# A VectorE no-op that takes the cross-engine waits of each scan group in a four-layer scan network

## The chip, the cores and the metric

The kernel runs on one core of a Trainium2 chip. A core has a matrix engine (TensorE, PE in the profile), three engines for elementwise work (VectorE = DVE, ScalarE = ACT, GpSimd = POOL) and a queue engine that issues the DMAs (SyncE = SP). [...] The metric is the device time of one execution in microseconds (us), as a median of several.

## What is computed

Four layers on images of 48 x 48 x 192, batch 4, all float32. Layers 0 to 3 are variants of the same thing, a selective scan over a sequence of tokens (layer 0 along 2304 tokens in both directions, layers 1 and 2 in four directions, layer 3 along rows and columns of 48). Cut to what matters here:

```python
delta = softplus(dt @ dtW.T + dtB)         # (L, D)
A = -exp(A_log)                            # (D, N), N = 16 states
def step(h, t):                            # t runs over the L tokens
    d_t, u_t, b_t, c_t = t
    h = exp(d_t[:, None] * A) * h + (d_t * u_t)[:, None] * b_t[None, :]
    return h, sum(h * c_t[None, :], -1)
_, ys = lax.scan(step, h0, (delta, xc, Bm, Cm))
y = ys + xc * D
```

For every channel d and state n there is thus a linear recurrence h = a * h + b over the tokens, with a = exp(delta * A), b = delta * u * B, and then a sum over n of h * C. Projections, short convolutions, norms and gates stand around it.

## The kernel before

**Tiling.** Channels lie on the 128 partitions, in three blocks i = 0, 1, 2. Tokens come in chunks of 384 (`CH`). The 16 states are taken in groups g of four (`NG`), so that one group is a tile of 128 x (4 x 385) or, where the scan starts anew in every row, 128 x (4 x 384). A *job* is one chunk in one direction. In layers 0 and 3 it has 3 x 4 = 12 groups; in layers 1 and 2 (`parts` = 2) two blocks of states share the partitions and a job has 6. Over the kernel there are 3456 groups: 1152 of layer 0, 1152 of layers 1 and 2, 1152 of layer 3.

**One group.** Its steps are methods of `ScanJob`:

- `fetch` (for i = 0 only): a DMA on SP's queue brings B and C of the group, broadcast over the partitions, into a tile `bcb`.
- `decay` (L367): four ScalarE exponentials write the tile `a`, one of three that are used in turn.
- `carry` (L384): in layers 0 to 2 GpSimd copies the state at the end of the chunk before into the first column of `bcb`.
- `enter` (L398), once for each i: ScalarE copies delta * u into the PSUM tile `du`, of which there is one.
- `scan` (L403): VectorE makes the *product* `inputs` = `du` * B (a TENSOR_TENSOR into PSUM) and then the *scan* `h` = scan(`a`, `inputs`) (a TENSOR_TENSOR_SCAN). `inputs` exists once, `h` in three buffers in layer 0 and four elsewhere.
- `weigh` (L421): GpSimd saves the last state (not in layer 3) and multiplies `h` by C in place.
- `reduce` (L435): TensorE sums `h` over the states into `y`, with an identity matrix as weights, four matmuls for a group.

**Order.** `run_jobs` (L737) writes the order out by hand. At step t it records: `scan` of group t, `decay` of group t + 2, `take` of y, `carry` for group t + 1, `weigh` of group t, then pieces of the next job's projections (`stream`) and of a norm (`side`), gates and drives on GpSimd, and `reduce` of group t - 1. `InOrder` (L48) and `in_order` (L95) keep each engine to that order. So GpSimd always has `carry` of group t + 1 just ahead of `weigh` of group t, and TensorE sums a group one step after it was scanned.

**Waits.** Nothing of the waits is written in the kernel: the framework finds for each instruction what it depends on, and leaves out a wait that an earlier instruction of the same engine has made already. [...] In the program as it is built, the stream of VectorE around a typical group of layer 0 reads

```
semaphore instruction   waits DVE (scan before)
TENSOR_TENSOR inputs    waits POOL (carry)
semaphore instruction   waits DVE (this product), PE (readers of the h buffer)
TENSOR_TENSOR_SCAN h    waits ACT (decay)
```

Where POOL and DMA waits are not needed, the product has the DVE wait in its own slot, with no semaphore instruction ahead of it: that is so for 736 of the 3456 products, most of them in layer 3.

Of the kernel before, what the change touches and what calls it, by code (L numbers as in the profile page):

```python
# [13 lines left out]
AF = mybir.ActivationFunctionType  # L14
ALU = mybir.AluOpType
# [11 lines left out]
NG = 4  # L27
# [20 lines left out]
class InOrder:  # L48


    def __init__(self, tc, engine):
        self.tc, self.engine = tc, engine
# [6 lines left out]
class K:  # L59
# [35 lines left out]
    def in_order(self, ins):  # L95
# [9 lines left out]
        self.last_act = ins.ins.name  # L105
        return ins

    def copy(self, out, in_):
        return self.act(out, in_, AF.Copy)

    def mm(self, out, pairs, start=True, stop=True, engine=None):
        n = len(pairs)
        for i, (lhsT, rhs) in enumerate(pairs):
            (engine or self.nc.tensor).matmul(  # L114
                out, lhsT, rhs, start=start and i == 0, stop=stop and i == n - 1
            )

    def mmo(self, out, pairs, start=True, stop=True):

        self.mm(out, pairs, start, stop, self.t)  # L120

    def rsqrt(self, out, in_, eps):

# [99 lines left out]
class ScanPools:  # L223
# [6 lines left out]
    def __init__(self, k, ctx, parts, rows):  # L230
        pool = k.tc.tile_pool
        self.parts, self.rows = parts, rows
        self.wide = 128 // parts
        self.n = N // parts
        self.groups = self.n // NG
        self.W = W = CH if rows else CH + 1
        self.one = ctx.enter_context(pool(name="one", bufs=1))
        self.two = ctx.enter_context(pool(name="two", bufs=2))
        self.bcs = ctx.enter_context(pool(name="bcs", bufs=5 if rows else 4))
        self.hs = ctx.enter_context(pool(name="hs", bufs=4 if rows or parts == 2 else 3))  # L240
        self.y = ctx.enter_context(pool(name="y", bufs=2 if rows else 1, space=PSUM))
        self.ps = ctx.enter_context(pool(name="ps", bufs=2, space=PSUM))
        self.vec = ctx.enter_context(pool(name="vec", bufs=1, space=PSUM))

        inputs = k.tile(self.vec, [128, 1536 if rows else 2048], "inputs")
        self.b = inputs[:, : NG * W].rearrange("p (j l) -> p j l", l=W)
        self.du = k.tile(self.vec, [128, 512], "du")[:, :W]
        self.ones = k.tile(self.one, [128, 1], "ones")
        k.nc.vector.memset(self.ones, 1.0)
        self.decays = [k.tile(self.one, [128, NG, W], f"a{i}") for i in range(3)]  # L250
        self.n_decays = 0
        self.revs = [None] * 3
        self.yts = 3 if rows else 2
        self.rev = None

        self.sum = k.ident
        if parts == 2:
            self.sum = k.tile(self.one, [128, 64], "sum")
            k.nc.vector.tensor_tensor(self.sum, k.ident[:, :64], k.ident[:, 64:], ALU.add)
# [28 lines left out]
class ScanJob:  # L288
# [10 lines left out]
    def __init__(self, k, pools, w, c0, rev, prev):  # L299
        self.k, self.pools, self.w, self.c0, self.rev, self.prev = k, pools, w, c0, rev, prev  # L300
        self.entry, self.tokens = pools.entry(rev)
        self.bcb = {}
        self.y = {}
        self.a = {}
        self.h = {}
        self.du = {}

    def unit(self, slots, rows, pairs, act):

        made = []  # L310

        def pe():
            ps = self.k.tile(self.pools.ps, [128, 512], "ps")[:rows, :CH]
            made.append(ps)
            out, pp = pairs(ps)
            self.k.mmo(out, pp)

        return slots, pe, lambda: act(made[0])
# [36 lines left out]
    def fetch(self, g):  # L355

        k, pools = self.k, self.pools
        wide = pools.wide
        self.bcb[g] = k.tile(pools.bcs, [128, 2, NG, pools.W], "bcb")
        for m in range(pools.parts):  # L360
            at = (m * pools.groups + g) * 2 * NG
            k.nc.sync.dma_start(
                self.bcb[g][m * wide : (m + 1) * wide].rearrange("p s j l -> p (s j l)"),
                self.bc[at : at + 2 * NG, :].rearrange("r l -> (r l)").partition_broadcast(wide),
            )

    def decay(self, i, g, between=None):  # L367

        k, w, pools = self.k, self.w, self.pools
        if i == 0:  # L370
            self.fetch(g)
        a = self.a[i, g] = pools.next_decays(k, self.rev)
        for j in range(NG):
            if j == NG - 1 and between is not None:
                between()
            out, in_ = a[:, j, self.tokens], self.delta[:, i, :]
            if pools.rows:
                lo = 0 if self.rev else 1
                out, in_ = (
                    v.rearrange("p (r l) -> p r l", l=S)[:, :, lo : lo + S - 1] for v in (out, in_)  # L380
                )
            k.act(out, in_, AF.Exp, scale=w.A[:, i, g * NG + j : g * NG + j + 1])

    def carry(self, i, g):  # L384

        if not self.pools.rows and self.prev is not None:
            at = self.entry
            self.k.g.tensor_copy(
                self.bcb[g][:, 0, :, at : at + 1].squeeze(2),
                self.prev.state[:, i, g * NG : (g + 1) * NG],  # L390
            )

    def drive(self, i):

        du = self.du[i] = self.k.tile(self.pools.two, [128, CH], "dus")
        self.k.g.tensor_tensor(du, self.delta[:, i, :], self.xs[:, i, :], ALU.mult)

    def enter(self, i):  # L398

        self.pools.turn(self.k, self.rev)  # L400
        self.k.copy(self.pools.du[:, self.tokens], self.du.pop(i))

    def scan(self, i, g):  # L403

        k, pools = self.k, self.pools
        b, du, W = pools.b, pools.du, pools.W
        k.v.tensor_tensor(
            b, du.unsqueeze(1).to_broadcast([128, NG, W]), self.bcb[g][:, 0, :, :], ALU.mult
        )
        step = -1 if self.rev else 1  # L410
        h = self.h[i, g] = k.tile(pools.hs, [128, NG, W], "h")
        k.v.tensor_tensor_scan(
            h.rearrange("p j l -> p (j l)")[:, ::step],
            self.a.pop((i, g)).rearrange("p j l -> p (j l)")[:, ::step],
            b.rearrange("p j l -> p (j l)")[:, ::step],
            0.0,
            ALU.mult,
            ALU.add,
        )

    def weigh(self, i, g):  # L421

        k, pools = self.k, self.pools
        h = self.h[i, g]
        if not pools.rows:
            if g == 0 and i == 0:
                self.state = k.tile(pools.two, [128, 3, pools.n], "state")
            last = 0 if self.rev else CH
            k.g.tensor_copy(
                self.state[:, i, g * NG : (g + 1) * NG], h[:, :, last : last + 1].squeeze(2)  # L430
            )
        ht = h[:, :, self.tokens]
        k.g.tensor_tensor(ht, ht, self.bcb[g][:, 1, :, self.tokens], ALU.mult)

    def reduce(self, i, g):  # L435

        k, pools = self.k, self.pools
        if g == 0:
            self.y[i] = k.tile(pools.y, [128, 512], "y")[: pools.wide, :CH]
            self.skip(i)  # L440
        h = self.h.pop((i, g))
        for j in range(NG):
            n = g * NG + j
            k.mmo(
                self.y[i],
                [(pools.sum, h[:, j, self.tokens])],
                start=n == 0 and not self.skips,
                stop=n == pools.n - 1,
            )


class DirJob(ScanJob):
# [1382 lines left out]
```

## Time and profile before

| what | value |
|---|---|
| median of 3 runs | 19676.89 us (19675.04 to 19686.36) |
| the profiled execution's own time | 19685.32 us |
| its span, first to last instruction | 19683.5 us |
| granted TensorE clock | 0.942 |
| VectorE busy | 18085.6 us (92%) |
| PE / ACT / POOL busy | 17478.0 (89%) / 12836.3 (65%) / 14746.8 (75%) us |
| HBM traffic | 117 GB/s over the span, queue q1 41.3% of 16 engines |

The first and last groups of the three scan stages start at 36.0 and 6239.1 us (layer 0), 6715.8 and 12941.5 us (layers 1 and 2), 13108.5 and 19221.7 us (layer 3). Between them stand a stage of convolutions and the loading of layer 3, and an MLP comes last.

How to read the profile: a group's line gives line of code, engine, operation, output <- inputs by tile name, shape and number; then busy time, mean ns of one, and after the second bar the idle time of the engine just before those instructions and what ended most of it. As every recorded operation goes through the helper in L56 or L93, tiles tell the groups apart, not lines. A timeline's line gives start, duration, engine, operation, and in brackets the idle time before it, where it is long enough to be named. Semaphore instructions are in the trace, with start and duration, but not in the views.

### The profile page before, as it was taken

How to read it: one execution, taken by the hardware profiler on the slowest of the kernel's cores; microseconds unless marked ns; L12 is line 12 of the kernel's file. 1: busy time of each engine (PE TensorE's matmuls, PEld its weight loads, DVE VectorE, ACT ScalarE, POOL GpSimd, SP SyncE). 2: the span in 40 equal slices, each digit the busy share in tenths (PEclk: the TensorE clock that was granted, in tenths of full speed). 3: DMA queues.
4: the chain of work that ended last, by engine and by line, in shares of the span. 5: the costliest groups of instructions: out<-in, count | busy, mean ns of one | idle time of the engine just before them, and what ended most of it. 6: DMA issues, size and time to landing. Idle time of an engine off the chain costs nothing.

```text
span 19683.5 us, 159587 instructions
## 1 busy us (share of the span) xinstructions
PE 17478.0 (89%) x48240; PEld 8281.7 (42%) x48240; DVE 18085.6 (92%) x7297; ACT 12836.3 (65%) x22582; POOL 14746.8 (75%) x10860
## 2 busy tenths in 40 slices
PE   8999999999998878888888888889999999998989
PEld 4544545444444322233233333334444444444444
DVE  8999999999997699999999999969999999999993
ACT  6766767666665466666666766756666666666663
POOL 7888888878876378888888888857777777777770
PEclk9999999999999989999999999989999999999999
DMA  3333333323323366666666666633222232333221
GB/s 114 115 116 109 118 118 116 116 103 114 115 102 98 95 135 140 148 146 146 146 144 145 138 146 145 138 107 108 105 103 104 105 110 100 110 107 108 104 106 46
DMA packets 500475, 2306.35 MB, mean 117 GB/s; under 512 B 76664, under 2 KB 334304, under 8 KB 347168
## 3 DMA queue, kind: packets, MB, share of 16 engines
q1 hardware_dynamic: 499616, 2296.14, 41.3%
q8 instruction: 387, 6.34, 0.1%
q14 instruction: 472, 3.87, 0.1%
HBM read 2103.60 MB, written 192.32 MB: 117 GB/s over the span
## 4 chain that ended last, share of the span: by engine, by line
DVE 43%; POOL 26%; PE 15%; issue 8%; ACT 5%; DMA 1%; DVEq 1%; POOLq 0%; SPq 0%; ACTq 0%
DVE h L56 28%; POOL h L56 20%; DVE inputs L56 15%; PE y L56 7%; PE ps L56 5%; POOL dus L56 2%; ACT a L93 2%; PE vps L114 2%; POOL state L56 1%; ACT L93 1%; PE mop L114 1%; DMA bcb<-bc 1%; POOL yt L56 1%; PE mps L114 1%; POOL bcb L56 1%
## 5 line engine op out<-in xcount | busy, mean ns | idle before, releaser
L56 POOL TENSOR_TENSOR h<-h,bcb 128x1536 f32<-128x1536 f32 x3456 | 11907.9, 3446 | 1715.9 <-DVE h L56 1440.0
L56 DVE TENSOR_TENSOR_SCAN h<-a,inputs 128x1540 f32<-128x1540 f32 (+1 forms) x3456 | 11609.4, 3359 | 448.2 <-ACT a L93 9.4
L93 ACT ACTIVATE a<-delta,A 128x384 f32<-128x384 f32 (+1 forms) x13824 | 7435.8, 603 | 3166.6 <-DVE h L56 3155.1
L56 PE MATMUL y<-h,ident 128*128 128x384 f32 x18432 | 6776.7, 516 | 509.7 <-POOL h L56 506.3
L56 DVE TENSOR_TENSOR inputs<-du,bcb 128x1540 f32<-128x1540 f32 (+1 forms) x3456 | 6115.4, 1769 | 467.2 <-ACT du L93 88.7
L56 PEld LDWEIGHTS y<-h,ident 128*128 128x128 f32 x18432 | 3620.4, 201 | 3513.4 <-POOL h L56 974.4
L56 PE MATMUL y<-h,sum 128*64 128x384 f32 x9216 | 3652.7, 545 | 595.0 <-POOL h L56 477.7
L56 PEld LDWEIGHTS y<-h,sum 128*64 128x64 f32 x9216 | 1291.4, 150 | 2915.3 <-issue 1756.0
L56 POOL COPY state<-h 128x4 f32<-128x4 f32 x2304 | 431.6, 187 | 2190.7 <-DVE h L56 2144.2
L56 PE MATMUL ps<-xh,diag 128*128 128x384 f32 x4032 | 1419.0, 491 | 185.1 <-ACT xc L93 185.1
L56 PE MATMUL ps<-u,inT 96*128 96x384 f32 x3456 | 1265.6, 497 | 178.8 <-ACT z L93 133.1
L56 PE MATMUL ps<-bcd,dtT 12*128 12x384 f32 (+1 forms) x2304 | 1017.6, 549 | 394.1 <-ACT delta L93 391.2
L56 PEld LDWEIGHTS ps<-xh,diag 128*128 128x128 f32 x4032 | 750.2, 189 | 779.5 <-ACT xc L93 273.2
L93 ACT ACT_TABLE_LOAD x794 | 1018.7, 1283 | 14.6
L90 ACT ACT_TABLE_LOAD x789 | 1012.3, 1283 | 14.7 <-PEq L1825 0.7
L56 PEld LDWEIGHTS ps<-u,inT 96*128 96x128 f32 x3456 | 652.7, 192 | 694.3 <-ACT z L93 211.7
L93 ACT ACTIVATE delta<-ps,vec 128x384 f32<-128x384 f32 x1152 | 631.7, 579 | 298.2 <-PE ps L56 291.2
L56 PE MATMUL ps<-yt,outT 128*96 128x384 f32 x2304 | 789.7, 486 | 0.4 <-POOL yt L56 0.4
L56 PEld LDWEIGHTS ps<-bcd,dtT 12*128 12x128 f32 (+1 forms) x2304 | 383.0, 192 | 965.2 <-ACT delta L93 628.6
L93 ACT ACTIVATE du<-dus 128x384 f32<-128x384 f32 x1152 | 557.9, 484 | 151.3 <-DVE inputs L56 145.8
L56 POOL TENSOR_TENSOR dus<-delta,xc 128x384 f32<-128x384 f32 x576 | 574.7, 998 | 49.8 <-ACT delta L93 49.8
L93 ACT ACTIVATE o<-ps 96x384 f32<-96x384 f32 x288 | 140.3, 487 | 687.8 <-PE ps L56 687.8
(131 smaller groups left out, 9694.4 us busy)
## 6 DMA issues: line engine op xcount, KB each, us to landing
bcb<-bc SPq DMA_DIRECT2D x384, 1540.0 KB
bcb<-bc SPq DMA_DIRECT2D x768, 770.0 KB
bcb<-bc SPq DMA_DIRECT2D x384, 1536.0 KB
y<-o SPq DMA_DIRECT2D x192, 288.0 KB
xs<-xi_wh SPq DMA_DIRECT2D x96, 288.0 KB
xs<-xi_hw SPq DMA_DIRECT2D x96, 288.0 KB
added<-y SPq DMA_DIRECT2D x96, 288.0 KB
xs<-x_wh SPq DMA_DIRECT2D x96, 288.0 KB
```

Source lines behind the costliest of these rows:

```text
L56: return lambda *a, **kw: self.tc.keep_in_program_order(op(*a, **kw))
L90: self.in_order(self.nc.scalar.preload_act_table_set(LOG_EXP))
L93: return self.in_order(self.nc.scalar.activation(out, in_, func, **kw))
L114: (engine or self.nc.tensor).matmul(out, lhsT, rhs, start=start and i == 0, stop=stop and i == n - 1)
```

## The change

Ahead of each group's product a no-op of VectorE is recorded (`engine_nop`[...]). It is given, by hand, a dependency on everything of another engine that the product or the scan waits for: the last exponential of the group's `decay` and, for i = 0, the DMAs of `fetch`; the `carry` copy; the `enter` copy of ScalarE for the first group of a block; and, for the `h` buffer about to be overwritten, the last matmul that read it and the GpSimd multiplication that wrote it. As the no-op has made those waits, the framework leaves them out at the product and the scan, which keep their wait for VectorE itself.

```diff
+    def gather(self, waits):
+        nop = self.v.engine_nop()
+        for ins in waits:
+            self.tc.add_manual_dep(
+                nop.ins,
+                ins.ins.name,
+                mybir.DependencyInfo(
+                    mybir.DependencyClass.Sync, mybir.DependencyReason.DATA
+                ),
+                reason="gathered waits",
+            )
...
     def decay(self, i, g, between=None):
...
-            k.act(out, in_, AF.Exp, scale=w.A[:, i, g * NG + j : g * NG + j + 1])
+            ins = k.act(out, in_, AF.Exp, scale=w.A[:, i, g * NG + j : g * NG + j + 1])
+        self.waits[i, g] = [ins, *(self.fetched[g] if i == 0 else [])]
...
     def scan(self, i, g):
...
+        waits = self.waits.pop((i, g))
+        if g == 0:
+            waits.append(pools.entered)
+        if pools.n_h >= pools.hbufs:
+            of = pools.n_h - pools.hbufs
+            waits += [pools.readers[of], pools.weighed[of]]
+        pools.n_h += 1
+        k.gather(waits)
         k.v.tensor_tensor(
             b, du.unsqueeze(1).to_broadcast([128, NG, W]), self.bcb[g][:, 0, :, :], ALU.mult
         )
...
     def weigh(self, i, g):
...
-        k.g.tensor_tensor(ht, ht, self.bcb[g][:, 1, :, self.tokens], ALU.mult)
+        ins = k.g.tensor_tensor(ht, ht, self.bcb[g][:, 1, :, self.tokens], ALU.mult)
+        pools.weighed.append(ins)
...
     def reduce(self, i, g):
...
-            k.mmo(
+            ins = k.mmo(
                 self.y[i],
                 [(pools.sum, h[:, j, self.tokens])],
                 start=n == 0 and not self.skips,
                 stop=n == pools.n - 1,
             )
+        pools.readers.append(ins)
```

In the program as it is built, the stream of VectorE around the same group then reads

```
semaphore instruction   waits PE (readers of the h buffer), ACT (decay)
ENGINE_NOP              waits POOL (carry)
TENSOR_TENSOR inputs    waits DVE (scan before)
TENSOR_TENSOR_SCAN h    waits DVE (this product)
```

The order of PE's, ACT's and POOL's working instructions is unchanged; on SP's queue a DMA of `bcb` and one of `prior` change places in 112 positions of 3431. Semaphore instructions on VectorE fall from 7673 to 4680, with 3456 no-ops added. On ScalarE they rise from 2862 to 4645 and on GpSimd from 3382 to 4245: some instructions there now also name a wait that they got implied before, such as ScalarE's wait for its own earlier write of `a`, or GpSimd's for the readers of `h` in layer 3.

More of the change, by code (lines that the diff above doesn't have):

```diff
@@ L113, in mm @@
         for i, (lhsT, rhs) in enumerate(pairs):
-            (engine or self.nc.tensor).matmul(
+            ins = (engine or self.nc.tensor).matmul(
                 out, lhsT, rhs, start=start and i == 0, stop=stop and i == n - 1
             )
+        return ins
     def mmo(self, out, pairs, start=True, stop=True):
-        self.mm(out, pairs, start, stop, self.t)
+        return self.mm(out, pairs, start, stop, self.t)
     def rsqrt(self, out, in_, eps):
@@ L239, in __init__ @@
         self.bcs = ctx.enter_context(pool(name="bcs", bufs=5 if rows else 4))
-        self.hs = ctx.enter_context(pool(name="hs", bufs=4 if rows or parts == 2 else 3))
+        self.hbufs = 4 if rows or parts == 2 else 3
+        self.hs = ctx.enter_context(pool(name="hs", bufs=self.hbufs))
         self.y = ctx.enter_context(pool(name="y", bufs=2 if rows else 1, space=PSUM))
@@ L251, in __init__ @@
         self.n_decays = 0
+        self.readers = []
+        self.weighed = []
+        self.n_h = 0
+        self.entered = None
         self.revs = [None] * 3
@@ L302, in __init__ @@
         self.bcb = {}
+        self.fetched = {}
         self.y = {}
@@ L306, in __init__ @@
         self.du = {}
+        self.waits = {}
     def unit(self, slots, rows, pairs, act):
@@ L359, in fetch @@
         self.bcb[g] = k.tile(pools.bcs, [128, 2, NG, pools.W], "bcb")
+        self.fetched[g] = []
         for m in range(pools.parts):
             at = (m * pools.groups + g) * 2 * NG
-            k.nc.sync.dma_start(
+            ins = k.nc.sync.dma_start(
                 self.bcb[g][m * wide : (m + 1) * wide].rearrange("p s j l -> p (s j l)"),
@@ L365, in fetch @@
             )
+            self.fetched[g].append(ins)
     def decay(self, i, g, between=None):
@@ L387, in carry @@
             at = self.entry
-            self.k.g.tensor_copy(
+            ins = self.k.g.tensor_copy(
                 self.bcb[g][:, 0, :, at : at + 1].squeeze(2),
@@ L391, in carry @@
             )
+            self.waits[i, g].append(ins)
     def drive(self, i):
@@ L400, in enter @@
         self.pools.turn(self.k, self.rev)
-        self.k.copy(self.pools.du[:, self.tokens], self.du.pop(i))
+        self.pools.entered = self.k.copy(self.pools.du[:, self.tokens], self.du.pop(i))
     def scan(self, i, g):
```

## The prediction, on record before the changed kernel ran

> **What bounds the kernel now.** I read the page first, its busy line and its costliest groups.
>
> ```profile
> PE 17478.0 (89%) x48240; PEld 8281.7 (42%) x48240; DVE 18085.6 (92%) x7297; ACT 12836.3 (65%) x22582; POOL 14746.8 (75%) x10860
> ...
> L56 DVE TENSOR_TENSOR_SCAN h<-a,inputs 128x1540 f32<-128x1540 f32 (+1 forms) x3456 | 11609.4, 3359 | 448.2 <-ACT a L93 9.4 <-DVE inputs L56 7.1 <-PE ps L56 1.9
> L56 DVE TENSOR_TENSOR inputs<-du,bcb 128x1540 f32<-128x1540 f32 (+1 forms) x3456 | 6115.4, 1769 | 467.2 <-ACT du L93 88.7 <-POOL bcb L56 51.3 <-DVE h L56 45.3
> ```
>
> Product and scan take 17725 of VectorE's 18086 us. The idle ahead of them is 448.2 + 467.2 = 915 us, and the releasers named explain a fifth of it: most is a small gap at each instruction. The same seen by stage, in windows inside layer 0, layers 1 and 2, and layer 3:
>
> ```profile
> 200.00:6200.00 6000.00, 5541.39 (x15854) 2917.68 (x15853) 5716.73 (x2228) 4103.38 (x7191) 4884.06 (x4069) 0.97 0.33 113
> 6800.00:12900.00 6100.00, 5179.13 (x13414) 1847.00 (x13413) 5790.68 (x2257) 4133.25 (x7486) 4926.04 (x4204) 0.92 0.65 143
> 13200.00:19200.00 6000.00, 5416.96 (x15213) 2873.37 (x15212) 5786.04 (x2261) 3873.13 (x6678) 4515.31 (x2276) 0.94 0.30 106
> ```
>
> The columns after the length are PE, PEld, DVE, ACT, POOL: VectorE is busy 95, 95 and 96% in all three; ACT and POOL are well below; PE's busy time is padded by pipelining (its matmuls start 0.32 us apart but are drawn 0.49 long, so at that spacing it is 87, 74 and 83% full). So a group costs VectorE 1.77 + 3.36 + two gaps, and the group's period, from one product's start to the next, is 5.39, 5.41 and 5.31 us in the stages. The gaps are what can be gained. The timeline of VectorE in layer 3 shows their two sizes:
>
> ```profile
> 15000.49 1.77 DVE L56 TENSOR_TENSOR inputs<-du,bcb 128x1536 f32<-128x1536 f32 x1
> 15002.38 3.35 DVE L56 TENSOR_TENSOR_SCAN h<-a,inputs 128x1536 f32<-128x1536 f32 x1
> 15005.77 1.77 DVE L56 TENSOR_TENSOR inputs<-du,bcb 128x1536 f32<-128x1536 f32 x1
> ```
>
> From the product's end (15002.26) to the scan 0.12, from the scan's end (15005.73) to the next product 0.04. This product has its VectorE wait in its own slot; the scan has semaphore instructions ahead of it[...]. Sorted by the form of the waits, the trace has these gaps (medians, nearly without spread):
> - wait for VectorE in the own slot: 34.5 ns (1104 products);
> - wait for VectorE on a semaphore instruction, one wait there: 103 to 105 ns (1088 products, 766 scans); with a DMA wait too: 91 (541 products); with a PE or ACT wait too: 131 to 133 (480 products, 2690 scans); on two semaphore instructions: 187 to 202 (240 products).
>
> [...]
>
> **Part 1: the gaps.** In the changed program all scans and all but 3 products have only the VectorE wait, in their own slot, so every gap should go to 34.5 ns.
> - Product to scan: 2690 x (131.5 - 34.5) + 766 x (103 - 34.5) = 261 + 52 = 313 us.
> - Scan to product: 1088 x 69.5 + 480 x 98.5 + 541 x 56.5 + 240 x 158 = 76 + 47 + 31 + 38 = 191 us. The 1104 gain nothing.
> Together 505 us. Behind this lies some more: 18 us of the scans' idle time are scattered holes of about 0.35 us for which no releaser was late; [...]I let 15 of them go.
>
> **Part 2: the no-op.** Its semaphore instruction and its own wait are dealt with while the scan before runs (3.36 us)[...]. What isn't covered is its time in the engine, between scan and product. The cheapest thing that VectorE does in this trace is a one-element memset:
>
> ```profile
> 1.35 0.06 DVE L1189 MEMSET eps<- 96x1 f32 x1
> 1.36 0.06 DVE L1190 MEMSET eps<- 96x1 f32 x1
> 1.37 0.06 DVE L249 MEMSET ones<- 128x1 f32 x1
> ```
>
> They take 0.06 each but start 0.01 apart, and two instructions of VectorE with no open wait between them start about 80 ns ahead of the former's end (60 pairs in L1099). So a no-op can slip into the last 80 ns of the scan, while the product behind it must wait for the scan's end anyway. Lower bound 0. Upper bounds: 59 ns in series (the memset's whole record), or, if the no-op waits for the scan and the product then for it, a small operation's whole record (157 ns, TENSOR_TENSOR of 2 elements in L1022) and another 34.5. I take 0.
>
> **Part 3: the waits moved ahead.** The scan's waits for `a` and for the `h` buffer now hold the product, 1.8 us earlier. Group by group I set the end of the last ACT, PE and POOL instruction that the no-op names against the end of the scan before. `a` is early by 6 us in the median, because `decay` runs two groups ahead; apart from the three stage starts, the few late ACT arrivals were the product's own (`du`). The readers of `h` are late in 33 groups, all in layer 0 (three buffers), by 36 us in all, where the wait was hidden under the product before. That is +36. Behind the no-op stand product and scan, and behind these `weigh` and `reduce`, so the delay isn't hidden.
>
> **Part 4: late arrivals that stay.** POOL's `carry` comes after the scan in 125 groups (48 us in all), since a longer GpSimd operation stood before it; `du` in 36 (43 us); these stay, as do about 27 us of DMA. With every period 0.15 us shorter they come later by 0.15 to 0.3: about 230 groups with PE's, so +40. POOL's next cluster, some 480 groups early by 0.4 to 0.5, stays on the safe side. Where a wait is late, no-op and product are now handed over one after the other: 180 x 0.07 = +13.
>
> **Part 5: the rest.** The extra semaphore instructions on ACT stand ahead of the first exponential of a group, those on POOL ahead of `weigh` in layer 3. Both follow VectorE's end, about 0.07 to 0.1 us each, but ACT has 3155 us of idle time for `h` before these exponentials, and POOL's results in layer 3 are 12 us early: nothing. The exchanged DMAs: nothing, `bcb` is 2 us early or more in nine of ten groups (the exceptions are in the 27 us).
>
> Sum: -505 - 15 + 36 + 40 + 13 = -431 us. Against the profiled execution, 19685.3 us (span 19683.5), that is 19254; the median of the runs is 8 below, so 19246. New period about 5.2 us plus late arrivals.
>
> **Rivals.**
> - *The no-op stands in series*, 59 ns in each group: +204, so 19450. For it: no trace shows a no-op. Against: the memsets 0.01 apart. The gap from scan to product would read about 0.09.
> - *Another engine becomes the bound* in layers 0 to 2: POOL is 26% of the chain that ended last and PE 15%. Then only layer 3 gains, 112 + 19 = 131 us: 19546. Against: POOL is 81% busy there and `carry` is early in all but 125 of 1920 groups.
> - *Slower: the no-op serialises the engine.* If it starts after the scan has ended and the product after it has, a group pays up to 157 + 34.5 = 0.19 us: +660, so 19906. It decides from 431 / 3456 = 0.125 us for each no-op: above that the product's gap exceeds what both gaps lost. [...] Against: tiny operations without a wait overlap.
> - *That the waits don't move* is excluded by the built program.
>
> **How the numbers follow.** Main forecast 0.71, no-op in series 0.12, another bound 0.05, serialising 0.09, something that cancels to nothing 0.03. A measurement of this kernel can tell about 0.2% (40 us) from no change. Faster: 0.71 + 0.12 + 0.05 = 0.88; the same 0.03; slower 0.09. The main case alone spans 19160 (no growth of lateness, and all holes gone) to 19400 (twice the growth, a no-op of 20 ns); with the series case the range is 19160 to 19470.
>
> **What would show it.** Scan gaps of 0.03 to 0.04 in the timeline in all stages, idle before the scans down from 448 to about 120 us, and before the products from 467 to about 350; periods near 5.2; ACT and POOL as busy in us as before. Scan gaps still at 0.13 would make part 1 wrong; product gaps above 0.1 would show the no-op; new waits of the product for `y` or `ps` in layer 0 would show part 3 bigger than I made it.

## The result and the profile after

The changed kernel takes 19348.26 us (median of 4 runs, 19327.21 to 19359.67) against 19675.97 us: a ratio of 0.9831, 95% interval 0.9814 to 0.9848. The profiled execution took 19327.21 us, the fastest of the four, 358 us less than that of before. The forecast was 19246 us with a range of 19160 to 19470, so the direction and the range held, and about a quarter of the forecast gain is missing.

The page of the changed kernel, its busy line and VectorE's two groups:

```profile
PE 17368.5 (90%) x48240; PEld 8258.1 (43%) x48240; DVE 18080.4 (94%) x7297; ACT 12819.5 (66%) x22582; POOL 14759.7 (76%) x10860
...
L56 DVE TENSOR_TENSOR_SCAN h<-a,inputs 128x1540 f32<-128x1540 f32 (+1 forms) x3456 | 11607.0, 3359 | 145.2 <-DVE inputs L56 1.4
...
L56 DVE TENSOR_TENSOR inputs<-du,bcb 128x1540 f32<-128x1540 f32 (+1 forms) x3456 | 6112.7, 1769 | 413.2 <-ACT a L93 116.9
```

Busy times are unchanged to 0.7%. The idle time before the scans went from 448.2 to 145.2 us, nearly as forecast (120). That before the products went only from 467.2 to 413.2 us (forecast about 350), and it has a new releaser, ACT `a`. VectorE's timeline in layer 3 shows the new gaps:

```profile
15000.65 1.77 DVE L56 TENSOR_TENSOR inputs<-du,bcb 128x1536 f32<-128x1536 f32 x1
15002.52 3.35 DVE L56 TENSOR_TENSOR_SCAN h<-a,inputs 128x1536 f32<-128x1536 f32 x1
15005.91 1.77 DVE L56 TENSOR_TENSOR inputs<-du,bcb 128x1536 f32<-128x1536 f32 x1
15007.78 3.35 DVE L56 TENSOR_TENSOR_SCAN h<-a,inputs 128x1536 f32<-128x1536 f32 x1
15011.17 1.77 DVE L56 TENSOR_TENSOR inputs<-du,bcb 128x1536 f32<-128x1536 f32 x1
15012.97 3.35 DVE L56 TENSOR_TENSOR_SCAN h<-a,inputs 128x1536 f32<-128x1536 f32 x1
```

Every product here starts 0.04 us after the scan before it ends. The last scan here starts 0.03 after its product (15012.94 to 15012.97), as most do: in the trace 3074 of the 3456 scans have a median gap of 34 ns. But the two scans ahead of it still have 0.10. They are of the 382 whose gap is 103 ns in the median: these have kept a wait for GpSimd, and with it a semaphore instruction. (In this trace no instruction of VectorE names more than one wait; of the 4680 semaphore instructions 1204 name one and 3476 two.) GpSimd clears a column of the decay tile where the direction of the scan changes (`next_decays`, L288 of the changed kernel), and the change does not name that memset to the no-op.

From the first product's start to the last, the stages shrank from 6203 to 6115 us (layer 0), 6226 to 6070 (layers 1 and 2) and 6113 to 5992 (layer 3): by 88, 156 and 121 us, layer 0 by the least. Its timeline on VectorE has stretches like this one, and the windows below it are of the same stretch (columns: window, length, then busy us of PE, PEld, DVE, ACT, POOL, then TensorE's granted clock):

```profile
3005.74 1.77 DVE L56 TENSOR_TENSOR inputs<-du,bcb 128x1540 f32<-128x1540 f32 x1
3007.55 3.36 DVE L56 TENSOR_TENSOR_SCAN h<-a,inputs 128x1540 f32<-128x1540 f32 x1
3013.53 1.77 DVE L56 TENSOR_TENSOR inputs<-du,bcb 128x1540 f32<-128x1540 f32 x1 [2.63 <-ACT a L93]
```

```profile
3007.00:3013.50 6.50, 6.50 (x11) 3.20 (x10) 3.87 (x2) 5.50 (x11) 6.42 (x6) 0.50 0.12 8
2997.00:3007.00 10.00, 9.16 (x28) 4.78 (x27) 9.86 (x5) 8.31 (x15) 9.10 (x10) 1.00 0.06 12
```

TensorE's clock is at 0.50 for these 6.5 us, against 1.00 in the 10 us before, and its sums of `h` start 0.64 us apart in place of 0.32. The product, which needs nothing of TensorE, now waits for them, because the no-op ahead of it does. The bracket names ACT `a`, but by the trace the exponentials that this group needs were done at 3004.66 and GpSimd's copy at 3011.53; the matmuls that read the `h` buffer ended at 3013.37. So the releaser that a view names for a wait on several engines has to be checked. I set, group by group, the ends of all that the no-op names against the end of the scan before: in layer 0, 69 products wait for `h`'s readers, 103 us in all, and 41 for GpSimd, 24 us; in layers 1 and 2, 40 wait for ACT (43 us) and 46 for GpSimd (35 us).

### The profile page after: what moved, and what is told of

Same layout as the page of the kernel before. It is cut to its first block, busy times and chain, and to the rows that moved or that the text cites. A ratio compares the mean times of both kernels' runs of the same rounds, so it can differ in the third digit from the quotient of the medians.

```text
span 19325.4 us, 162699 instructions
## 1 busy us (share of the span) xinstructions
PE 17368.5 (90%) x48240; PEld 8258.1 (43%) x48240; DVE 18080.4 (94%) x7297; ACT 12819.5 (66%) x22582; POOL 14759.7 (76%) x10860
## 4 chain that ended last, share of the span: by engine, by line
DVE 41%; POOL 32%; PE 13%; issue 9%; ACT 3%; DMA 2%; SPq 0%; POOLq 0%; DVEq 0%; ACTq 0%
DVE h L56 27%; POOL h L56 25%; DVE inputs L56 14%; PE y L56 6%; PE ps L56 4%; POOL dus L56 2%; PE vps L128 2%; POOL state L56 1%; ACT a L93 1%; DMA bcb<-bc 1%; POOL yt L56 1%; POOL bcb L56 1%; PE mop L128 1%; PE mps L128 1%; POOL nx L56 1%
## 5 line engine op out<-in xcount | busy, mean ns | idle before, releaser
L56 DVE TENSOR_TENSOR_SCAN h<-a,inputs 128x1540 f32<-128x1540 f32 (+1 forms) x3456 | 11607.0, 3359 | 145.2 <-DVE inputs L56 1.4
L56 DVE TENSOR_TENSOR inputs<-du,bcb 128x1540 f32<-128x1540 f32 (+1 forms) x3456 | 6112.7, 1769 | 413.2 <-ACT a L93 116.9
```

The lines of the kernel that those rows point to most:

```text
L56: return lambda *a, **kw: self.tc.keep_in_program_order(op(*a, **kw))
```

## The experiments

Two questions: do the gaps behave as the sum had it, and what took the missing part? First theory: the readers of `h`, moved ahead of the product, and the 382 scans. Rivals: a no-op costs time in the engine; or the other engines can't keep the faster pace, wherever the wait stands.

**The changed kernel again**, as yardstick for the runs beside it.

> The changed kernel once more, beside the other runs of this call, as their yardstick. Both theories: about 19348 us, scattered by some 30 us, scan gaps of 34 ns.

Measured: 19335.61 us (19324.99 to 19364.86), ratio 0.9828 (0.9812 to 0.9845). In layer 0, 65 products wait for `h`'s readers, 92 us in all, much as in the first series.

**One part at a time.** In the first kernel (scan_only) the no-op stands between product and scan and takes the scan's waits, with the memset's among them; in the second (product_only) it stands ahead of the product and takes the product's alone.

```diff
-        self.waits[i, g] = [ins, *(self.fetched[g] if i == 0 else [])]
+        self.waits[i, g] = [*self.fetched[g]] if i == 0 else []
+        self.held[i, g] = [ins, pools.cleared[(pools.n_decays - 1) % 3]]
...
-            waits += [pools.readers[of], pools.weighed[of]]
+            held += [pools.readers[of], pools.weighed[of]]
...
-        k.gather(waits)
         k.v.tensor_tensor(
             b, du.unsqueeze(1).to_broadcast([128, NG, W]), self.bcb[g][:, 0, :, :], ALU.mult
         )
+        k.gather(held)
```

This is the first kernel's edit; `pools.cleared` holds the memsets of the three decay tiles. The second has the same lists, but leaves `k.gather(waits)` where it was, skips it where `waits` is empty (2720 no-ops are left), and gathers `held` nowhere.

> One part of the change alone: the no-op stands between product and scan and takes the scan's waits; the product keeps its own waits and semaphore instructions as before. Theory 1 (each gap is the time of handing over after the wait, and gaps add up): product to scan goes to 34 ns in all 3456 groups, 313 us and some 15 us of holes less than before, scan to product unchanged, some growth of late arrivals: near 19360 us (19340 to 19390). Theory 2 (the cross-engine waits matter, not where VectorE's own wait stands): the scan's waits were all early, so no gain, 19676 us.

> The other part alone: the no-op ahead of the product takes the product's waits, the scan keeps its own waits and semaphore instructions as before. Theory 1: scan to product goes to 34 ns where nothing is late, 191 us less than before, product to scan stays at 131 ns, growth of late arrivals 10 us: near 19495 us (19475 to 19520). Theory 2 (cross-engine waits matter): 19676 us less what was late, which a no-op can't take away, so 19676 us.

Measured: 19386.07 us (ratio 0.9850, 0.9836 to 0.9865) and 19519.44 us (0.9918, 0.9904 to 0.9933): 296 and 162 us less than before, where the sums of gaps gave 313 + 15 and 191. The page of the first, then of the second:

```profile
L56 DVE TENSOR_TENSOR_SCAN h<-a,inputs 128x1540 f32<-128x1540 f32 (+1 forms) x3456 | 11607.0, 3358 | 124.3 <-ACT a L93 4.1
...
L56 DVE TENSOR_TENSOR inputs<-du,bcb 128x1540 f32<-128x1540 f32 (+1 forms) x3456 | 6114.5, 1769 | 492.9 <-ACT du L93 95.6
```

```profile
L56 DVE TENSOR_TENSOR_SCAN h<-a,inputs 128x1540 f32<-128x1540 f32 (+1 forms) x3456 | 11610.7, 3360 | 442.8 <-ACT a L93 5.6
...
L56 DVE TENSOR_TENSOR inputs<-du,bcb 128x1540 f32<-128x1540 f32 (+1 forms) x3456 | 6114.7, 1769 | 304.6 <-POOL bcb L56 71.2
```

Each no-op emptied the idle time of its own instruction alone: 448 to 124 us of the scans, 467 to 305 us of the products. That speaks for the theory that it matters where VectorE's wait for itself stands; a scan's cross-engine waits were early before, and moving them still gained 296 us. Each run falls some 30 us short of its sum: late arrivals grew with the pace, by more than I had allowed (the products' idle time rose by 26 us in the first; in the second their waits for `du`, `a`, `bcb` and its DMA went from 163 to 190 us).

**Both parts, with a no-op each.** The lists are those of the kernels just shown: `waits` has carry, `du` and DMA, `held` has decay, memset and the users of `h`.

```diff
         k.gather(waits)
         k.v.tensor_tensor(
             b, du.unsqueeze(1).to_broadcast([128, NG, W]), self.bcb[g][:, 0, :, :], ALU.mult
         )
+        k.gather(held)
```

> Two no-ops for each group: the first, ahead of the product, takes the product's waits alone (carry, du, DMA), the second, between product and scan, those of the scan (decay, the readers of the h buffer, and GpSimd's memset of the decay tile, which 382 scans of the changed kernel still name themselves). Theory 1 (what is missing of the forecast is the readers of h, moved ahead of the product in layer 0: 69 late groups, 103 us, and the 382 scans with a GpSimd wait, 26 us): the product covers most of the late readers again, so 75 to 100 us less in layer 0 and 26 us less elsewhere, near 19235 us (19215 to 19265). Theory 2 (the readers are late whatever waits for them, since TensorE can't keep the faster pace): the same time is lost ahead of the scan in place of the product, near 19320 us. Theory 3 (a no-op costs time in the engine): the second one adds as much as the first, gaps above 34 ns, 19380 us or more.

Measured: 19238.91 us (19230.93 to 19248.63), ratio 0.9776 (0.9761 to 0.9791): what theory 1 gave, and 97 us below the changed kernel beside it. The longest waits of VectorE around the groups (us in total, times, longest):

```profile
DVE inputs L56 <- ACT du L93: 105.7, 36, 32.8
...
DVE inputs L56 <- POOL bcb L56: 80.8, 119, 2.7
...
DVE inputs L56 <- DMA bcb<-bc: 25.0, 4, 21.6
DVE h L56 <- PE y L56: 13.0, 19, 1.5
```

The readers cost 13 us at the scan in place of some 100 at the product. They aren't fewer: by the trace they end after the scan before in 104 groups of layer 0, 106 us in all, against 89 and 99 us in the changed kernel. The product's 1.77 us cover most of that again. Theory 2 falls; theory 3 too, since the gaps are 34 ns on both sides.

**Which of the moved waits.** Two no-ops again, with the scan's waits parted: in the first kernel only the users of `h` stand behind the product, in the second they stand ahead of it, and `decay` and memset behind.

Against two_nops, readers_behind and then rest_behind:

```diff
-        self.waits[i, g] = [*self.fetched[g]] if i == 0 else []
-        self.held[i, g] = [ins, pools.cleared[(pools.n_decays - 1) % 3]]
+        self.waits[i, g] = [ins, pools.cleared[(pools.n_decays - 1) % 3]]
+        self.waits[i, g] += self.fetched[g] if i == 0 else []
+        self.held[i, g] = []
```

```diff
-            held += [pools.readers[of], pools.weighed[of]]
+            waits += [pools.readers[of], pools.weighed[of]]
```

> Two no-ops, but the second one, between product and scan, holds only the waits for the former users of the h buffer (TensorE's sum and GpSimd's multiplication); decay and the memset of the decay tile are waited for ahead of the product. Theory 1 (of the waits moved ahead of the product only the readers of h cost time): as fast as two_nops, 19239 us (19220 to 19260). Theory 2 (the decay wait ahead of the product costs as well): between that and 19310 us, with the product idle for ACT a.

> The complement: two no-ops, the readers of h are waited for ahead of the product as in the changed kernel, and the second no-op, between product and scan, holds decay and the memset of the decay tile. Theory 1: it keeps the loss of the readers and wins only the 382 scans with a GpSimd wait, 26 us: near 19310 us (19290 to 19330), with 60 to 70 late products in layer 0 and the scatter from run to run of the changed kernel. Theory 2 (the decay wait ahead of the product costs): clearly below 19290 us.

Measured: 19241.49 us (19240.67 to 19242.97; ratio 0.9777, 0.9762 to 0.9791) and 19314.67 us (19278.79 to 19334.67; 0.9810, 0.9793 to 0.9826). The waits of the second:

```profile
DVE inputs L56 <- PE y L56: 129.2, 73, 2.7
...
DVE inputs L56 <- ACT du L93: 75.2, 34, 27.8
...
DVE inputs L56 <- POOL bcb L56: 63.6, 87, 4.4
```

With `decay` out of the way the profile itself names `y`, 129 us in 73 products. So it was the users of `h` alone, and of these TensorE's sums, since GpSimd's multiplication ends 6 us or more ahead in every group of layer 0: `decay` ahead of the product costs nothing that shows. The scatter seems to go with them too: 32 and 40 us between the slowest and the fastest run of the changed kernel and 56 in rest_behind, but 2 in readers_behind and 18 in two_nops. With four runs of each this is a hint and not more.

**The price of a no-op**, 15 more of them, without waits, behind the first.

```diff
         k.gather(waits)
+        for _ in range(15):
+            k.v.engine_nop()
```

> The changed kernel with 15 further no-ops, without waits, behind each group's first one: it measures what one no-op costs in the engine. Theory 1 (a no-op takes some 10 ns like the one-element memsets, and the first few slip into the last 80 ns of the scan): the product's gap grows from 34 ns to about 34 + 16 x 10 - 100 = 95 ns, some 60 ns for each group, 200 us in all, near 19550 us (19400 to 19700). Theory 2 (each stands in series with a small operation's record of 59 ns): 15 x 59 ns, 0.9 us for each group, 3000 us more. [...]

Measured: 19516.54 us (ratio 0.9916, 0.9901 to 0.9930), 181 us above the changed kernel of the series before. In layer 3:

```profile
15000.42 1.76 DVE L56 TENSOR_TENSOR inputs<-du,bcb 128x1536 f32<-128x1536 f32 x1
15002.21 3.35 DVE L56 TENSOR_TENSOR_SCAN h<-a,inputs 128x1536 f32<-128x1536 f32 x1
15005.66 1.76 DVE L56 TENSOR_TENSOR inputs<-du,bcb 128x1536 f32<-128x1536 f32 x1
```

The product's gap grew from 34 to 97 ns. In the trace a no-op has a record of 13 ns; most start 7 or 8 ns apart. In layer 3 the first three start 75, 68 and 60 ns ahead of the scan's end, and the fourth only at its end. So one is hidden, and 15 more show 63 ns. That is theory 1, with 7 or 8 ns in place of 10 for each. In all, the products' idle time is 204 us above that of the run after_again, and their own records are 14 us shorter. The scatter of these runs is 12 us, though the readers of `h` stand ahead of the product here too.

**TensorE's order.** If the readers of `h` are late because they stand behind projections, they can go ahead of them.

```diff
+        if 0 <= t - behind < len(groups):
+            job, i, g = groups[t - behind]
+            job.reduce(i, g)
         stream.run(at if at < per - 1 else per)
...
-        if 0 <= t - behind < len(groups):
-            job, i, g = groups[t - behind]
-            job.reduce(i, g)
```

> The changed kernel (one no-op) with the sum of group t - 1 placed ahead of step t's projections on TensorE in place of behind them; nothing else changes. Theory 1 (the readers of h come late in layer 0 because they stand behind projections on a TensorE that is at half clock in these moments): they come earlier, most of the 90 to 100 us of waits for them goes, near 19260 us; projections start later, which may cost up to 20 us elsewhere. Theory 2 (TensorE at half clock is too slow whatever its order): the same 19340 us, the product still waits for y in some 65 groups of layer 0.

Measured: 22135.28 us, ratio 1.1248 (1.1229 to 1.1267): both theories missed. The longest waits, all engines:

```profile
POOL state L56 <- DVE h L56: 4109.4, 2175, 15.4
...
DVE inputs L56 <- ACT du L93: 2470.0, 625, 9.6
ACT bcd L93 <- PE ps L56: 1943.1, 383, 9.7
```

The sum waits for GpSimd's multiplication (`y` for `h`: 1168.2 us, 672 times), and the projections now wait behind it. Through `bcd`, `delta` and `du`, which are made from them, that delays the next job's first products by up to 9.6 us. The projections, not the sums, have the shorter lead here. In layer 0 the readers of `h` still come late in 81 groups, by 125 us, at a slower pace; with so much mixed in, the run doesn't say what an earlier sum alone would bring.

**The carries**, the largest group of late arrivals left in two_nops apart from the stage's start: for i = 1 and 2 the copy is made one step earlier.

```diff
-            if t + 1 < len(groups):
-                job, i, g = groups[t + 1]
-                job.carry(i, g)
+            for s in (1, 2):
+                if t + s < len(groups) and (groups[t + s][1] == 0) == (s == 1):
+                    job, i, g = groups[t + s]
+                    job.carry(i, g)
```

> Two no-ops, as in two_nops, and for the blocks i = 1 and 2 the carry copy of group t + 2 ahead of the multiplication of group t, one step earlier than before. Theory 1 (late carries are what is left of GpSimd, 72 late groups of layer 0 with i = 1 or 2, 38 us): near 19200 us, with no POOL wait left in layer 0 ahead of the product; the 47 late groups of layers 1 and 2, all of i = 0, stay. Theory 2 (these waits only hide others, such as TensorE's readers): 19239 us, with the time at the scan's wait for y.

Measured: 19219.73 us (19214.50 to 19225.79), ratio 0.9766 (0.9751 to 0.9780), the fastest version of all.

```profile
DVE inputs L56 <- POOL bcb L56: 40.9, 49, 2.1
DVE h L56 <- PE y L56: 29.1, 27, 2.8
```

Half of each theory: the waits for the carry fell by 40 us, to the 49 products of layers 1 and 2, and 16 us of that came back at the readers of `h`. The median is 19 us below that of two_nops, which ran in an earlier series; the two intervals overlap.

## Why the prediction was right, and where its size was off

Against the profiled execution's -358 us, by the prediction's parts:

- *Part 1, the gaps (-505).* Right, but for "In the changed program all scans and all but 3 products have only the VectorE wait": 382 scans keep GpSimd's, 382 x 68.5 ns = 26 us. The built program showed it. The holes at the scans went from 18 to 1 us, about as assumed (-15). The gaps sorted by the form of the wait carry this part: 3074 scans whose one wait is in their own slot have 34 ns, 382 with a semaphore instruction left have 103, and the one-part runs bear the sum out. Why the place of the wait makes the difference was not shown.
- *Part 2, the no-op (0).* Right. The semaphore instruction ahead of the no-op ended before the scan did in 96% of the groups, by 3.2 us in the median. The no-op's record is 13 ns, it starts 75 ns ahead of the scan's end where nothing is late (3247 groups), and gaps of 34 ns exclude both the rival of 59 ns in series and that of a serialised engine. But it takes time of VectorE itself: of 16 in a row the fourth starts only when the scan has ended, and the product's gap grows to 97 ns.
- *Part 3, the moved waits (+36).* Its mechanism was right and this term was mis-sized: 103 us in the profiled run, 92 in the run beside it. I counted the readers that were late at the old pace and took that number over to the new one.

  Call margin the time by which the readers of the buffer end ahead of the end of the scan before. In layer 0 the sum of group t - 3 has the time from the end of its own scan to the end of scan t - 1, two periods, and a period is 0.17 us shorter; so my estimate from these traces is a margin smaller by 0.34 us. There, taken at full clock, the median margin falls by 0.31 to 0.41 us in the first five of the twelve groups of a job. But from the sixth group to the tenth the fall is 0.32, 0.49, 0.66, 0.83 and 1.00 us, one more 0.17 for each group, as if TensorE's stream kept its own time there while VectorE ran ahead.

  And at the tenth group TensorE is mostly at half clock. There lie 67 of the 89 late groups and 92 of their 99 us; the product at 3013.53 shown above is one. In 66 of the 96 jobs before, and 69 of 96 after, the clock was at half within the 9 us ahead of the scan's end. At full clock the margin there was 2.00 us in the median before and 1.00 after, and no group late; at half clock it was 0.31 us before, with 24 late, and -1.1 us after, with 67 late. So the clock is much as it was, and the margin that had covered it is gone. Part 4's 0.15 to 0.3 for each late group added time to those already late and none for those that became late.
- *Part 4, late arrivals (+40 and +13).* In the waits, ACT and GpSimd grew from 71 to 102 us: +31, the hand-over included, less than forecast though the readers are left out. The hand-over of a late wait depends on where it stands: from the end of the late instruction to the product it takes 167 ns for TensorE, whose wait is on the semaphore instruction, but 40 ns for GpSimd, whose wait is in the no-op's own slot (33 ns before the change, on the product). ScalarE's `du` shows both: 120 ns with its wait on the semaphore instruction (34 products), 39 ns in the own slot (5). The forecast's 0.07 us for each was an estimate; 69 late ones of the first kind make some 9 us, near the 13 in all.
- *Part 5 (0).* Right as far as seen: no stage shows a new wait for ACT's first exponential or for `weigh`. The 0.07 to 0.1 us for each semaphore instruction on ACT and GpSimd was an estimate.
- *Readings beside the sum.* By the trace before, `du`'s 36 late groups are late by 26 us in all, not 43; `a` is early by 7.8 us in the median, not 6; and matmuls 0.32 us apart fill 85, 70 and 81% of the three windows, not 87, 74 and 83. No term of the sum rests on these.

Together -505 + 26 - 17 + 103 + 31 = -362, near the 365 by which the three stages shrank. The medians differ by 328 us, because the profiled run of the changed kernel was the fastest of its four and that of the kernel before was 9 us above its median.

What stays open: why TensorE's clock falls at that place of the job, and why its stream doesn't follow the pace from the sixth group on. At the tenth group program and order are the same, and half clock parts the late groups from those in time: 67 of 69 late at half, none of 27 at full. That is a comparison inside one trace (in the second run of this kernel 61 of 62 and none of 34); no run here changed the clock alone.

## What to carry to other kernels

Where two dependent instructions of one engine follow each other, try to keep the second one's wait for the first in its own slot: here its gap was then 34 ns, against 91 to 202 ns in the trace before with that wait on semaphore instructions. The other waits were gathered on a no-op ahead of it, which here added nothing to the gap and brought some 90 ns for each of about 5400 instructions. But gather for each instruction only what that instruction needs: a wait that is moved ahead of a neighbour loses the neighbour's duration as cover, here the product's 1.77 us. And before counting which waits are late, take from every margin what the faster pace will take, place by place: here it was some 0.35 us in the first groups of a job and 1.0 in the tenth, which had the least to spare when TensorE was at half clock.

## What was not expected of the hardware

TensorE's clock falls to 0.50 for stretches of some us (the window above) in a stage whose mean is 0.97, and nearly always at the same place: of 73 such stretches that start in layer 0 of the changed kernel, 69 start between the ninth product of a job and the tenth, and 61 of 65 in its second run. The stage's mean hides that in 69 of its 96 jobs one group of twelve has a TensorE at half clock. Of 16 no-ops in a row only three start while the scan ahead of them, of 3.35 us, is still running, in its last 75 ns.
